# Self attention of a decoder layer: the softmax sums taken by ScalarE's accumulator from the first round's scores, in place of products with ones

## The chip, the cores and the metric

The kernel runs on 1 core of one Trainium2 chip. The metric is the device time of one execution in microseconds. Before the change the median of six executions is 4011.06 us (4002.22 to 4021.87). The profile and all times "in order of time" below come from one further execution, which took 4023.55 us with a span of 4021.6 us.

## The reference, cut to what matters

A decoder layer in float32: self attention, cross attention, a mixture of experts. Only self attention is touched. It is a differential attention over 32 sequences (b) of 128 tokens with 512 features, 16 heads of two halves ("sides") each, 16 features wide; a causal mask; for each side a softmax over the keys, and the second side's weights, times a scalar, are subtracted from the first's.

```python
q = (x @ Wq).reshape(b, t, 2 * H, HD).transpose(0, 2, 1, 3) * scaling
k = (x @ Wk).reshape(b, t, 2 * H, HD).transpose(0, 2, 1, 3)
v = (x @ Wv).reshape(b, t, H, 2 * HD).transpose(0, 2, 1, 3)
scores = jnp.einsum('bhqd,bhkd->bhqk', q, k)
aw = jax.nn.softmax((scores + causal).astype(jnp.float32), axis=-1)
aw = aw.reshape(b, H, 2, t, t)
aw = aw[:, :, 0] - lam * aw[:, :, 1]
attn = jnp.einsum('bhqk,bhkd->bhqd', aw, v)
attn = attn * jax.lax.rsqrt(jnp.mean(attn * attn, axis=-1, keepdims=True) + 1e-05)
```

## The kernel before, in words

`self_attention` handles one sequence b in two steps (cp = 0 and 1), eight heads a step, so there are 64 steps, and one step in two finishes a sequence. A step works on 4 head groups j (32 partitions each) times 2 chunks c times 2 sides: 16 score matrices of 128 queries by 128 keys. The scores are computed twice:

- First round, `maxima` (L231): eight products (L238) give scores with queries on partitions, in two PSUM buffers. VectorE (DVE in the profile) adds the causal mask and writes them to the SBUF tile `s` (L244), then takes the negated maximum of each row into `nm` (L251). `s` is read by nothing else.
- `turn_maxima` (L256): TensorE (PE) transposes `nm` (L262), and DVE puts the maxima into spare rows of the queries, `qm` (L264), so that the second round's products come out with the maximum already subtracted.
- Second round, `exponentials` (L270): 16 products (L279) give scores with keys on partitions; ScalarE (ACT) takes the exponential out of PSUM into `e`, two instructions (L286); GpSimd (POOL) zeroes what the mask excludes, two selects (L289).
- `weigh` (L294): eight products of `e` with the values (L303), and eight with `ones` (L309), which give the sum of the exponentials of each query. All land in one PSUM buffer `po`; DVE transposes it in blocks of 32 into `u` (L314).
- `divide` (L319): reciprocal of the sums (L323), the scalar for the second side (L324), and the product with the weighted values into `o` (L327).
- `finish` (L333), once a sequence: sum of the sides `at` on POOL (L338), squares `sq` on ACT (L342), their sums `ms` and a scaling on DVE (L344, L345), the power -0.5 `rr` on POOL (L347); `scale_out` gives `an` on DVE (L353), `turn_out` transposes it to `anT` (L361), `leave` multiplies by `wo` (L374) and adds the residual into `xres` (L378).

Beside these a step projects queries and keys of the next group of two sequences (`queries_and_keys`: products L207, evacuated by ACT to `kz` and `qT`, L213 and L218, and by POOL to `k1`, L214), projects values in every second step (`values`: L225, evacuated by ACT, L229), and normalizes and transposes inputs (`measure` with the moments of L56 to L66, `normalize` L74, `turn_in` L83 and L194).

The loop at the end of `self_attention` is a pipeline over steps n: step n does the maxima of step n, the exponentials of n - 1, weighing and dividing of n - 2, and so on up to `leave` of n - 5. The order on each engine is made from this program order by a scheduler that may move instructions; within an engine the instructions then run in that order, each waiting for semaphores of others. All PSUM results come from one pool of four buffers of two banks each, handed out in rotation, so a new product may have to wait for whoever empties the buffer used four requests earlier. In the last eight steps parts of cross attention are already mixed in.

Of the kernel before, what the change touches and what calls it, by code (L numbers as in the profile page):

```python
# [10 lines left out]
F32 = mybir.dt.float32  # L11
I32 = mybir.dt.int32
AF = mybir.ActivationFunctionType
# [5 lines left out]
P = 128  # L19
# [83 lines left out]
def self_attention(cm, x, x1_d, Wq, Wk, Wv, Wo, lq1, lk1, lq2, lk2, heads, heads_in, beside):  # L103
# [14 lines left out]
    nc, tc, bank = cm.nc, cm.tc, cm.banks  # L118
    B = x.shape[0]
    H, D, G = 16, 32, 2  # L120
    CP = 2
    ROW = (16, 0)
    with ExitStack() as ctx:
        wp = ctx.enter_context(tc.tile_pool(name="a_w", bufs=1))
        p1 = ctx.enter_context(tc.tile_pool(name="a_p1", bufs=1))
        p2 = ctx.enter_context(tc.tile_pool(name="a_p2", bufs=2))
# [44 lines left out]
        nc.scalar.activation(begun, cm.mhalf[:, 0:1], AF.Exp)  # L171

        hT, qT, kz, k1, vs = {}, {}, {}, {}, {}
        h, qm, expd, u, o, an = {}, {}, {}, {}, {}, {}

        def measure(b):
            if b < B:
# [42 lines left out]
        def values(g, i):  # L220
            if g * G >= B:
                return
            pv = bank()[:, 0, :]
            for ec in range(EC):
                nc.tensor.matmul(  # L225
                    pv, hT[g][:, ec, ts(i, P)], w["wv"][:, ec, :], start=ec == 0, stop=ec == EC - 1
                )
            vs[g, i] = p2.tile([P, E], F32, name="v", bufs=3)
            nc.scalar.copy(vs[g, i], pv)  # L229

        def maxima(b, cp):  # L231

            g, i = divmod(b, G)
            sc = [bank() for _ in range(2)]
            for c in range(CP):
                for j in range(4):
                    rows, oc = ts(j, 32), CP * cp + c
                    nc.tensor.matmul(  # L238
                        sc[j // 2][:, j % 2, ts(c, 2 * P)],
                        qT[g][rows, oc, i, :], kz[g, oc][rows, i], start=True, stop=True,  # L240
                    )
            s = p1.tile([P, 4, CP, 2, P], F32, name="s")
            for pair in range(2):
                nc.vector.tensor_tensor(  # L244
                    s[:, 2 * pair : 2 * pair + 2].rearrange("p j c s k -> p (j c s) k"),
                    sc[pair].rearrange("p j (x k) -> p (j x) k", k=P),
                    causal.unsqueeze(1).broadcast_to([P, 4 * CP, P]), ALU.add,
                )
            for side in range(2):
                at = nm[(CP * b + cp) % 2][:, side].rearrange("p (j r) -> p j r", r=32)  # L250
                nc.vector.tensor_reduce(  # L251
                    at[:, :, ROW[side] : ROW[side] + CP], s[:, :, :, side, :], AX.X, ALU.max,
                    negate=True,
                )

        def turn_maxima(b, cp):  # L256

            g, i = divmod(b, G)
            tr = bank()[:, 0, 0 : 2 * P].rearrange("p (s x) -> p s x", s=2)
            qm[b, cp] = p2.tile([P, 2, CP, P], F32, name="qm")  # L260
            for side in range(2):
                nc.tensor.transpose(tr[:, side], nm[(CP * b + cp) % 2][:, side], cm.ident)  # L262
            for side in range(2):
                nc.vector.scalar_tensor_tensor(  # L264
                    qm[b, cp][:, side], qT[g][:, CP * cp : CP * cp + CP, i, :],
                    others[:, side : side + 1],
                    tr[:, side].unsqueeze(1).broadcast_to([P, CP, P]), ALU.mult, ALU.add,
                )

        def exponentials(b, cp):  # L270

            g, i = divmod(b, G)
            sc = [bank() for _ in range(2)]
            q = qm.pop((b, cp))
            for c in range(CP):
                for side in range(2):
                    for j in range(4):
                        rows, oc = ts(j, 32), CP * cp + c
                        nc.tensor.matmul(  # L279
                            sc[j // 2][:, j % 2, ts(2 * c + side, P)],  # L280
                            k1[g, oc][rows, i, side, :], q[rows, side, c, :], start=True, stop=True,
                        )
            for pair in range(2):
                e = pe.tile([P, 2, CP, 2, P], F32, name="e")
                flat = e.rearrange("p j c s q -> p (j c s) q")
                nc.scalar.activation(  # L286
                    flat, sc[pair].rearrange("p j (x q) -> p (j x) q", q=P), AF.Exp
                )
                nc.gpsimd.affine_select(  # L289
                    out=flat, in_=flat, compare_op=ALU.is_ge, fill=0.0, base=0,  # L290
                    pattern=[[0, 4 * CP], [1, P]], channel_multiplier=-1,
                )
                expd[b, cp, pair] = e

        def weigh(b, cp):


            g, i = divmod(b, G)
            po = bank()
            es = [expd.pop((b, cp, pair)) for pair in range(2)]  # L300
            for c in range(CP):
                for j in range(4):
                    nc.tensor.matmul(  # L303
                        po[ts(j, 32), 0, ts(c, 2 * P)], vs[g, i][:, ts(4 * (CP * cp + c) + j, D)],
                        es[j // 2][:, j % 2, c], start=True, stop=True,
                    )
            for c in range(CP):
                for j in range(4):
                    nc.tensor.matmul(  # L309
                        po[ts(j, 32), 1, 0 : 2 * P], ones[:, c, :], es[j // 2][:, j % 2, c],  # L310
                        start=c == 0, stop=c == CP - 1,
                    )
            u[b, cp] = p1.tile([P, 6, 4, D], F32, name="u")
            nc.vector.transpose(  # L314
                u[b, cp].rearrange("p n k d -> p (n k d)"),
                po.rearrange("p two n -> p (two n)")[:, 0 : 6 * P],
            )

        def divide(b, cp):  # L319

            t = u.pop((b, cp))
            rs = p2.tile([P, CP, 2, 4], F32, name="rs")
            nc.vector.reciprocal(rs.rearrange("p c s k -> p s k c"), t[:, 4:6, :, 0:CP])  # L323
            nc.vector.tensor_scalar(rs[:, :, 1, :], rs[:, :, 1, :], nlam, None, ALU.mult)  # L324
            if cp == 0:
                o[b] = p1.tile([P, 2 * CP, 2, 4 * D], F32, name="o")
            nc.vector.tensor_tensor(  # L327
                o[b][:, CP * cp : CP * cp + CP].rearrange("p c s (k d) -> p (c s k) d", d=D),
                t[:, 0:4].rearrange("p n k d -> p (n k) d"),
                rs.rearrange("p c s k -> p (c s k)").unsqueeze(2).broadcast_to([P, 8 * CP, D]),  # L330
                ALU.mult,
            )
# [64 lines left out]
            )  # L397
        nc.vector.tensor_scalar(others, others, -1.0, 1.0, ALU.mult, ALU.add)


        ones = wp.tile([P, CP, D], F32, name="a_ones")
        nc.vector.memset(ones, 0.0)
        for c in range(CP):
            nc.vector.memset(ones[:, c, c : c + 1], 1.0)

        for b in range(G):
            measure(b)

# [9 lines left out]


        nm = [wp.tile([P, 2, P], F32, name=f"a_nm{i}") for i in range(2)]  # L420
        for t in nm:
            nc.gpsimd.memset(t, 0.0)

        for b in range(G):
# [26 lines left out]
        for n in range(len(steps) + 5):  # L451
            g, k = divmod(n, 2 * G)
            if n == len(steps) - 2 * G:
                early.close()
            at = {ago: steps[n - ago] for ago in range(6) if 0 <= n - ago < len(steps)}
            if 1 in at:
                turn_maxima(*at[1])
            if 0 in at:
                maxima(*at[0])
            queries_and_keys(g + 1, k)  # L460
            if 1 in at:
                exponentials(*at[1])
            if 2 in at:
                weigh(*at[2])
            if k % 2:
                values(g + 1, k // 2)
            elif 5 in at:
                leave(at[5][0])
            if 3 in at and at[3][1]:
                scale_out(at[3][0])  # L470
            if 2 in at:
                divide(*at[2])
                if at[2][1]:
                    finish(at[2][0])
            b = (g + 2) * G + k // 2
            if k % 2 == 0:
                measure(b)
                if 4 in at:
                    load_again(at[4][0])
            else:  # L480
                normalize(b)
                turn_in(b)
                load(b + G)
                if 4 in at:
                    turn_out(at[4][0])
            if n in beside:
                beside[n]()


class CrossAttention:  # L490
# [19 lines left out]
    ROW = (16, 0)  # L510
# [1158 lines left out]
```

## Time and profile before

| | us |
|---|---|
| median of six executions | 4011.06 |
| lowest and highest | 4002.22, 4021.87 |
| profiled execution | 4023.55 |
| its span | 4021.6 |
| self attention alone | about 0 to 770 of the span |
| self attention with cross attention mixed in | about 770 to 860 |
| granted TensorE clock, mean over the span | 0.991 |
| L309, products with ones, mean of one record | 0.379 (two records a product, four products side by side) |
| L286, exponential 128 x 1024 on ACT | 1.021 |
| L314, transpose 128 x 768 on DVE | 0.978 |

A line of a group in the profile names the source line, the engine, the operation, output and inputs, the shapes, the count, then busy time in us and the mean of one in ns, then the idle time of the engine before them and who ended it. In the view in order of time a line has start and length in us, the engine, the source line, the operation, the count of merged records and, in brackets, the idle time ahead and its releaser. A float32 product shows as two records, a transpose as one.

### The profile page before, as it was taken

How to read it: one execution, taken by the hardware profiler on the slowest of the kernel's cores; microseconds unless marked ns; L12 is line 12 of the kernel's file. 1: busy time of each engine (PE TensorE's matmuls, PEld its weight loads, DVE VectorE, ACT ScalarE, POOL GpSimd, SP SyncE). 2: the span in 40 equal slices, each digit the busy share in tenths (PEclk: the TensorE clock that was granted, in tenths of full speed). 3: DMA queues.
4: the chain of work that ended last, by engine and by line, in shares of the span. 5: the costliest groups of instructions: out<-in, count | busy, mean ns of one | idle time of the engine just before them, and what ended most of it. 6: DMA issues, size and time to landing. Idle time of an engine off the chain costs nothing. (4 is left out here: it accounts for less than half of the span.)

```text
span 4021.6 us, 58171 instructions
## 1 busy us (share of the span) xinstructions
PE 3869.6 (96%) x20020; PEld 2029.2 (50%) x20020; DVE 2201.1 (55%) x3525; ACT 1191.4 (30%) x1696; POOL 2255.8 (56%) x2420
## 2 busy tenths in 40 slices
PE   8999999989999999999999999999999999999999
PEld 5666666533333333334445555555555555555444
DVE  5777777778888888888323333333333333333111
ACT  3333333235665555555301111111111111111000
POOL 4444444453666666665326777777777777775000
PEclk9999999989999999999999999999999999999999
DMA  3110110121111111111145767676766676676210
GB/s 107 33 33 27 33 32 27 33 84 40 59 56 51 48 48 48 48 45 37 61 135 140 178 153 182 140 187 147 173 156 164 163 176 152 160 165 152 85 63 32
DMA packets 285980, 387.22 MB, mean 96 GB/s; under 512 B 147888, under 2 KB 179248, under 8 KB 285616
## 3 DMA queue, kind: packets, MB, share of 16 engines
q0 software_dynamic: 62912, 109.85, 15.3%
q1 hardware_dynamic: 81792, 190.98, 14.9%
q10 hardware_dynamic: 140976, 82.60, 7.4%
q8 instruction: 162, 2.65, 0.3%
q14 instruction: 138, 1.13, 0.1%
HBM read 617.52 MB, written 143.07 MB: 189 GB/s over the span
## 5 line engine op out<-in xcount | busy, mean ns | idle before, releaser
L1381 POOL DMA_INDIRECT e_xr<-h_d,e_run_of x832 | 849.5, 1021 | 288.7 <-issue 263.6
L1411 DVE TENSOR_TENSOR e_gu<-e_act,ps 128x352 f32<-128x352 f32 x208 | 108.4, 521 | 994.2 <-ACT e_act L1410 557.0
L653 DVE TENSOR_REDUCE nm<-ps 128x2 f32<-128x1024 f32 x512 | 610.9, 1220 | 61.5 <-PE ps L649 55.6
L1442 PE MATMUL ps<-wd,e_guT 128*128 128x512 f32 (+1 forms) x1248 | 577.0, 598 | 30.9 <-ACT e_y L1446 12.0
L676 ACT ACTIVATE xp<-ps 128x1024 f32<-128x1024 f32 x512 | 510.3, 1022 | 282.3 <-PE ps L649 213.7
L672 PE MATMUL ps<-xqn,xk 32*128 32x512 f32 x2048 | 537.9, 623 | 20.2 <-ACT xp L676 19.6
L1406 PE MATMUL ps<-wg,e_xT 128*128 128x352 f32 x1664 | 529.9, 461 | 15.0 <-DMA wg<-in_L_ffn_w_gate_dram 11.3
L649 PE MATMUL ps<-xk,xq 32*128 32x512 f32 x2048 | 537.1, 628 | 1.5 <-DVE xres L378 1.4
L1406 PE MATMUL ps<-wu,e_xT 128*128 128x352 f32 x1664 | 528.9, 461 | 7.0 <-DMA wu<-in_L_ffn_w_up_dram 5.8
L1406 PEld LDWEIGHTS ps<-wg,e_xT 128*128 128x128 f32 x1664 | 315.2, 190 | 253.9 <-issue 112.5
L1447 POOL DMA_INDIRECT sum_d<-e_y,e_into x208 | 338.1, 1625 | 178.3 <-ACT e_y L1446 96.3
L1406 PEld LDWEIGHTS ps<-wu,e_xT 128*128 128x128 f32 x1664 | 316.8, 191 | 186.5 <-DMA wu<-in_L_ffn_w_up_dram 9.1
L1442 PEld LDWEIGHTS ps<-wd,e_guT 128*128 128x128 f32 (+1 forms) x1248 | 236.3, 191 | 285.5 <-issue 225.9
L1410 ACT ACTIVATE e_act<-ps 128x352 f32<-128x352 f32 x208 | 96.3, 463 | 949.4 <-PE ps L1406 390.8
L672 PEld LDWEIGHTS ps<-xqn,xk 32*128 32x128 f32 x2048 | 165.2, 183 | 243.2 <-ACT xp L676 99.2
L1446 ACT ACTIVATE e_y<-ps,e_weight 128x512 f32<-128x512 f32 x208 | 142.9, 687 | 421.2 <-PE ps L1442 248.1
L1432 DVE STREAM_TRANSPOSE e_guT<-e_gr 96x384 f32<-96x384 f32 (+1 forms) x416 | 230.4, 554 | 61.5 <-DMA e_gr<-e_gu_d 49.6
L687 PE MATMUL ps<-xp,v 128*32 128x512 f32 x2048 | 246.0, 598 | 8.8 <-ACT xp L676 8.7
L987 POOL DMA_INDIRECT table_d<-entry,at x192 | 196.5, 1023 | 71.2 <-issue 50.8
L1393 DVE STREAM_TRANSPOSE e_xT<-e_xr 128x512 f32<-128x512 f32 x208 | 226.5, 1089 | 12.5 <-DMA e_xr<-h_d,e_run_of 8.6
L214 POOL TENSOR_SCALAR k<-kz,a_keep,a_extra 128x256 f32<-128x256 f32 x128 | 69.8, 554 | 265.3 <-ACT kz L213 265.3
L649 PEld LDWEIGHTS ps<-xk,xq 32*128 32x128 f32 x2048 | 161.2, 183 | 31.0 <-issue 9.7
(267 smaller groups left out, 4963.8 us busy)
## 6 DMA issues: line engine op xcount, KB each, us to landing
wg<-in_L_ffn_w_gate_dram SPq DMA_DIRECT2D x208, 704.0 KB
wu<-in_L_ffn_w_up_dram SPq DMA_DIRECT2D x208, 704.0 KB
wd<-in_L_ffn_w_down_dram SPq DMA_DIRECT2D x208, 576.0 KB
e_gu_d<-e_gu ACTq DMA_DIRECT2D x208, 192.0 KB
e_gr<-e_gu_d ACTq DMA_DIRECT2D x208, 192.0 KB
wd<-in_L_ffn_w_down_dram SPq DMA_DIRECT2D x208, 128.0 KB
e_xr<-h_d,e_run_of POOLq DMA_INDIRECT x832
xres<-in_x_dram SPq DMA_DIRECT2D x32, 256.0 KB
```

What stands on the lines that cost most here:

```text
L649: self.nc.tensor.matmul(sc[:, i, :], q[rows, ts(c, P)], k[rows, :], start=True, stop=True)
L653: self.nc.vector.tensor_reduce(at[:, self.ROW[side], 2 * pair : 2 * pair + 2], sc, AX.X, ALU.max, negate=True)
L672: self.nc.tensor.matmul(sc[:, i, :], k[rows, ts(c, P)], q[rows, :], start=True, stop=True)
L676: self.nc.scalar.activation(e, sc, AF.Exp)
L687: self.nc.tensor.matmul(po[b, side][ts(j, 32), :], self.v2[b % 2][:, c, 2 * j + side, :], es[j // 2][:, j % 2, :], start=c == 0, stop=c == ...
L987: self.nc.gpsimd.indirect_dma_start(out=self.table_ds[k % 2][:, :], out_offset=bass.IndirectOffsetOnAxis(ap=self.at[b][:, k : k + 1], axis=0),
L1381: self.cm.nc.gpsimd.indirect_dma_start(out=xr[:, t, :], out_offset=None, in_=self.h3_d.rearrange("t (q f) -> (t q) f", q=self.Q), in_offse ...
L1393: self.cm.nc.vector.transpose(xT.rearrange("p c (t i) -> p c t i", t=self.Q), self.xr.pop(i).rearrange("p t (j c) -> p c t j", c=EC),)
L1406: nc.tensor.matmul(pgu[:, half, 0:M], t[:, c, :], w[:, c, :], start=c == 0, stop=c == EC - 1)
L1432: self.cm.nc.vector.transpose(t[rows, 0:n, :].rearrange("p c (t i) -> p c t i", t=self.Q), g[rows, :, 0 : 32 * n].rearrange("p t (j c) -> ...
L1442: nc.tensor.matmul(py, t[:n, c, :], self.wd[s][:n, c, :], start=c == 0, stop=c == len(M_CHUNKS) - 1)
L1447: nc.gpsimd.indirect_dma_start(out=self.sum_d[:, :], out_offset=bass.IndirectOffsetOnAxis(ap=self.into[:, i : i + 1], axis=0), in_=y[:, :] ...
```

## The change

The exponentials of the first round's scores are now taken too, from `s` in place, by ScalarE: 16 activations of 128 x 128 a step, one for each score matrix, with the negated maximum as bias (one value a partition) and the engine's accumulator giving the row's sum into a column of a new tile `sm` (two of them, used in turn). `weigh` transposes `sm` into the free bank of `po` with one TensorE transpose; the eight products with `ones` and the tile `ones` go. The DVE transpose into `u` is 640 columns wide in place of 768. `s` moves to a pool with two buffers. In program order the sums of chunk 0 come behind `turn_maxima`, those of chunk 1 behind `exponentials`, both for step n - 1.

```diff
-            s = p1.tile([P, 4, CP, 2, P], F32, name="s")
+            s = sc_of[b, cp] = p2.tile([P, 4, CP, 2, P], F32, name="s")
...
+        def sums(b, cp, c):
+            n = (CP * b + cp) % 2
+            s = sc_of[b, cp]
+            for j in range(4):
+                for side in range(2):
+                    at = 32 * j + ROW[side] + c
+                    to = 32 * j + 2 * c + side
+                    nc.scalar.activation(
+                        s[:, j, c, side, :], s[:, j, c, side, :], AF.Exp,
+                        bias=nm[n][:, side, at : at + 1], accum_out=sm[n][:, to : to + 1],
+                    )
+            if c == CP - 1:
+                del sc_of[b, cp]
...
-            for c in range(CP):
-                for j in range(4):
-                    nc.tensor.matmul(
-                        po[ts(j, 32), 1, 0 : 2 * P], ones[:, c, :], es[j // 2][:, j % 2, c],
-                        start=c == 0, stop=c == CP - 1,
-                    )
-            u[b, cp] = p1.tile([P, 6, 4, D], F32, name="u")
+            nc.tensor.transpose(po[:, 1, 0:P], sm[(CP * b + cp) % 2], cm.ident)
+            u[b, cp] = p1.tile([P, 5, 4, D], F32, name="u")
             nc.vector.transpose(
                 u[b, cp].rearrange("p n k d -> p (n k d)"),
-                po.rearrange("p two n -> p (two n)")[:, 0 : 6 * P],
+                po.rearrange("p two n -> p (two n)")[:, 0 : 5 * P],
             )
...
-            nc.vector.reciprocal(rs.rearrange("p c s k -> p s k c"), t[:, 4:6, :, 0:CP])
+            nc.vector.reciprocal(rs.rearrange("p c s k -> p k (c s)"), t[:, 4, :, 0 : 2 * CP])
...
+        sm = [wp.tile([P, P], F32, name=f"a_sm{i}") for i in range(2)]
+        for t in nm + sm:
             nc.gpsimd.memset(t, 0.0)
...
             if 1 in at:
                 turn_maxima(*at[1])
+                sums(*at[1], 0)
             if 0 in at:
                 maxima(*at[0])
             queries_and_keys(g + 1, k)
             if 1 in at:
                 exponentials(*at[1])
+                sums(*at[1], 1)
```

More of the change, by code (lines that the diff above doesn't have):

```diff
@@ L173, in self_attention @@
         hT, qT, kz, k1, vs = {}, {}, {}, {}, {}
-        h, qm, expd, u, o, an = {}, {}, {}, {}, {}, {}
+        h, sc_of, qm, expd, u, o, an = {}, {}, {}, {}, {}, {}, {}
         def measure(b):
@@ L398, in self_attention @@
         nc.vector.tensor_scalar(others, others, -1.0, 1.0, ALU.mult, ALU.add)
[L401 to L404, printed above, removed]
         for b in range(G):
@@ L420, in self_attention @@
         nm = [wp.tile([P, 2, P], F32, name=f"a_nm{i}") for i in range(2)]
-        for t in nm:
+        sm = [wp.tile([P, P], F32, name=f"a_sm{i}") for i in range(2)]
+        for t in nm + sm:
             nc.gpsimd.memset(t, 0.0)
```

## Prediction

> **What bounds the kernel now.** I read the page first (shares of busy time), then the table by stage, then the instructions in order of time over two steps of self attention, then the groups of ScalarE by form. The page says that TensorE is nearly always busy:
>
> ```profile
> PE 3869.6 (96%) x20020; PEld 2029.2 (50%) x20020; DVE 2201.1 (55%) x3525; ACT 1191.4 (30%) x1696; POOL 2255.8 (56%) x2420
> ```
>
> The table by stage (busy us and, in brackets, instructions of PE, PEld, DVE, ACT, POOL; then clock, DMA share, GB/s), cut to the steady part of self attention:
>
> ```profile
> 100.00:750.00 650.00, 635.51 (x5516) 406.31 (x5514) 501.54 (x711) 213.52 (x357) 288.42 (x299) 0.99 0.10 30
> ```
>
> PE 98%, ACT 33%. From this alone the change pays: it takes work from PE and gives it to an idle engine. The instructions in order of time say otherwise. The work repeats every two steps: L361's anT starts at 402.64 and again at 427.99, so a pair takes 25.35 us. From one pair (start, us, engine, line, operation, count):
>
> ```profile
> 408.74 0.98 DVE L314 STREAM_TRANSPOSE u<-ps 128x768 f32<-128x768 f32 x1 [0.78 <-PE ps L309]
> 409.76 0.26 DVE L323 RECIPROCAL rs<-u 128x16 f32<-128x16 f32 x1
> 410.05 0.23 DVE L324 TENSOR_SCALAR rs<-rs,nlam 128x8 f32<-128x8 f32 x1
> 410.32 0.69 DVE L327 TENSOR_TENSOR o<-u,rs 128x512 f32<-128x512 f32 x1
> 413.06 0.69 DVE L344 TENSOR_REDUCE ms<-sq 128x16 f32<-128x512 f32 x1 [2.04 <-ACT sq L342]
> ```
> ```profile
> 406.85 1.94 ACT L286 ACTIVATE e<-ps 128x1024 f32<-128x1024 f32 x2
> 407.63 1.05 PE L309 MATMUL ps<-e,a_ones 128*32 128x256 f32 x16
> 407.94 2.13 POOL L289 TENSOR_SCALAR_AFFINE_SELECT e<-e 128x1024 f32<-128x1024 f32 x2 [0.53 <-ACT e L286]
> 411.10 1.27 POOL L338 TENSOR_TENSOR at<-o 128x512 f32<-128x512 f32 x1 [1.02 <-DVE o L327]
> 412.39 0.63 ACT L342 ACTIVATE sq<-at 128x512 f32<-128x512 f32 x1 [3.61 <-POOL at L338]
> 414.03 2.92 POOL L347 TENSOR_TENSOR rr<-ms,mhalf 128x16 f32<-128x16 f32 x1 [1.67 <-DVE ms L345]
> 416.99 0.69 DVE L353 SCALAR_TENSOR_TENSOR an<-at,rr 128x512 f32<-128x512 f32 x1 [2.26 <-POOL rr L347]
> 418.26 1.76 PE L279 MATMUL ps<-qm,k 32*128 32x128 f32 x32
> 424.00 2.14 POOL L289 TENSOR_SCALAR_AFFINE_SELECT e<-e 128x1024 f32<-128x1024 f32 x2
> 424.28 0.84 DVE L324 TENSOR_SCALAR rs<-rs,nlam 128x8 f32<-128x8 f32 x1
> 425.16 1.53 DVE L327 TENSOR_TENSOR o<-u,rs 128x512 f32<-128x512 f32 x1
> 427.34 1.99 PE L207 MATMUL ps<-hT,wk 128*128 128x256 f32 x8 [0.39 <-DVE xres L378]
> ```
>
> PE's busy time holds waits. L279 takes 1.76 us in this step and 1.17 us at 405.64 in the step before, the same 32 records; L238 takes 1.79 at 412.89 and 1.15 at 400.45; and at 427.34 PE waits 0.39 for xres. That is 1.6 us of slack in each pair. What sets the pair is a ring: PE's exponential scores (405.64) → e on ACT (ends 408.8) → the select on POOL (407.94 to 410.07) → rs, o on DVE (410.05 to 411.01) → at on POOL (to 412.37) → sq on ACT → ms on DVE → rr on POOL (to 416.95) → an on DVE (416.99), behind which DVE is busy without a break to xres, which frees the bank for L207 at 427.34 → 3.65 us of projections → the next exponential scores (430.99 = 405.64 + 25.35).
>
> **The products with ones.** L309 starts at 407.63 and the next product at 408.61: 0.98 us of PE a step, two a pair. In their place is one transpose; the two of L262 stand 0.31 us apart from their successor (400.14 to 400.45), so 0.16 us, up to 0.3 with its entry: PE saves about 0.7 us a step. The ring does not go through L309 but beside it. With it gone u can start at 407.96 (end of DVE's reductions) and not 408.74, and takes 640 columns for 768 (0.98 × 5/6 = 0.82, by width). But rs would come at 409.05, inside the select. What happens then is in the other step: rs at 424.28, 0.28 us into a select, takes 0.84 us and not 0.23, and ends with the first select; o takes 1.53 and not 0.69, and ends 0.55 us after the second. So rs and o end at about 410.1 and 410.8, and 0.15 to 0.2 us of the 0.98 is kept. In the other step the select starts at 424.00, after ve on DVE, and holds rs whether u is 0.16 us shorter or not: nothing.
>
> The Trainium skill (SBUF — State Buffer, "Who interferes with whom") says of this that the pair of ports shared by VectorE and GpSimd is an exclusive lock, for two SBUF inputs or a two-port mode, and that the first to issue blocks the other. The rows above agree for rs and o. By its sentence that the order of issue decides, an earlier rs could also take the lock first, and the sum would then gain up to 0.8 us a pair; the sum here goes by the rows.
>
> **DVE's order.** As the changed kernel is built, DVE runs ms, one qm, then ms2 (L345) and the other qm; before it ran ms, ms2, qm, qm. The last steps of before have that order once: L344 at 793.25, L345 at 794.24, 0.99 us apart, against 413.06 to 413.78, 0.72. rr waits for ms2: +0.27 us a pair in the ring. bn_stats moves behind the reductions of its step; its aggregate then follows it at once: 0 to +0.15, I take +0.1. The second buffer for s takes a wait away that nobody shows; the wait of L244 for ScalarE is for sums of two steps ago, ended some 5 us or more ahead.
>
> **The 16 new activations a step.** Their own row is missing; alone, without accumulator, the nearest rows give it. ScalarE's groups by form:
>
> ```profile
> L213 ACT ACTIVATE kz<-ps,a_keep 128x256 f32<-128x256 f32 x128 | 53.6, 470 | 395.2 <-PE ps L207 395.1
> L218 ACT ACTIVATE qT<-ps 128x256 f32<-128x256 f32 x64 | 24.5, 383 | 0.0
> L342 ACT ACTIVATE sq<-at 128x512 f32<-128x512 f32 x32 | 20.2, 630 | 113.5 <-POOL at L338 113.5
> L905 ACT ACTIVATE score<-score 128x32 f32<-128x32 f32 x32 | 7.4, 230 | 39.9 <-DVE score L904 39.9
> L440 ACT ACTIVATE lam_exps<-lam_dots 128x2 f32<-128x2 f32 x1 | 0.2, 212 | 0.0
> ```
>
> sq less score: 400 ns for 480 columns, 0.833 a column; 128 columns from SBUF: 310. An operand per partition (kz less qT): +87, so 0.40 us. Neighbours overlap by 0.10 (two e take 1.94, one 1.021), so one every 0.30 us if the accumulator costs nothing: the low end. Should the sum need a second instruction to fetch it, the nearest row is ScalarE's shortest (212 ns). It cannot begin before its activation has ended, so it loses the overlap there, and I let the next activation overlap with it: 0.40 + 0.21 - 0.10 = 0.51. With no overlap at all: 0.61, the high end. I take 0.51, the case of the nearest row; no row shows an accumulator. The Trainium skill (VectorE: DVE Perf Modes, "Two Vector instructions with no wait between them") says of VectorE that an output of the accumulator is a second instruction; it says nothing of ScalarE, and no row shows it.
>
> ScalarE has 8.4 us a pair now (kz, kz, qT 1.10 and e, e 1.94 in each step; sq, v, hT, h 2.30): with 32 sums it is 18.0, 24.7 or 27.9 us, by 0.30, 0.51, 0.61, in 25.35. It runs in order, and as built a step with sq has seven sums between e and sq and nine between hT and h; the other step has sixteen between e and kz. Behind seven sums wait sq, v and hT, and on sq the ring. Free at 408.8 + 7 × 0.51 = 412.4; sq is due at 412.39 - 0.2: late by 0.2. The nine end at 414.2 + 4.6 = 418.8, h at 419.5, kz (due 418.4) late by 1.1: e then ends at 422.5 for 421.83, which POOL takes at 424.00 anyway, after ve. The sixteen end at 430.7, kz due 431.1. So at 0.51 ScalarE just keeps up.
>
> **Sum for a pair:** -0.2 (o) + 0.27 (ms2) + 0.1 (ve) + 0.2 (sq) = about +0.4 us. The steady part has (765 - 90) / 25.35 = 27 pairs: +11 us. The last steps (765 to 860) are bound by DVE and POOL waits; as built, sums stand ahead of e there (nine: 793.7 + 4.6 = 798.3 for 795.95) and of h, which now waits behind rot; 1.8 to 1.9 us products with ones at the low clock go. I take +5, between -3 and +10. All: +16 on the profiled execution (4023.55, span 4021.6), which is 12.5 above the median 4011.06 of six; on the median 4027.
>
> **Rivals.** A difference within 0.3% (12 us) cannot be told from none here.
> 1. ScalarE becomes the bound: above 0.55 us a sum, 8.4 + 32 × 0.55 = 26.0. At 0.61 the pair is 27.9 plus about 0.1: +2.6 × 27 = +70, tail +8: 4089. For: 0.61 is in the bounds, and the order has no slack. Against: neighbours overlap in every row. 0.28.
> 2. The other side, faster: PE's time counts after all. If rs and o take their turn ahead of the select, the ring shortens with PE; then 2 × 0.75 × 27 = 41 us go: 3970. For: 98% busy. Against: the waits inside L279, L238, L207 and rs's 0.84. It decides where rs starts before 409.0. 0.12.
> 3. The sums are cheap (0.30 to 0.42) and hidden, sq is not late: +0.17 × 27 + 3 = +8: 4019, no difference to be told. 0.18.
> Forecast: 0.42, itself 4013 to 4045, two thirds of it above 4023. Slower 0.28 + 0.28 = 0.56; same 0.14 + 0.18 = 0.32; faster 0.12. That the sums go to another engine or the products stay is ruled out by the instructions as built. The range 3998 to 4085 leaves out most of rival 2 and the top of rival 1.
>
> **What would show it.** Right: pairs of about 25.8 us, PE's L207 waiting about 1 us or more for xres where it waited 0.39, rs held by the select in both steps, sq starting right behind the seventh sum, ACT 90% busy or more. Wrong: pairs of 24 us with rs free of the select (rival 2); kz and e starting right behind sums, POOL and PE waiting for e, pairs over 26.5 us (rival 1); sq waiting for POOL as now (rival 3). A sum slower than 0.61 us would break the upper end.

## The result, and the profile after

The changed kernel takes 4019.87 us (median of 35 runs, 4002.70 to 4031.98) where the kernel before, measured beside it, takes 4009.01 us (72 runs, 3994.11 to 4021.87). The ratio is 1.0024, with a 95% interval of 1.0017 to 1.0031: slower by 0.24%, less than the 0.3% that the prediction called the edge of what can be told, but with an interval that lies above one. The profiled execution of the changed kernel took 4010.80 us (span 4008.8); that of before took 4023.55. So the two traces stand the other way round from the medians, and only stretches of them are compared here, not their ends.

The page of the changed kernel (busy time, share of the span and instructions of each engine), and from the table by stage the same stretch as before (busy us and instructions of PE, PEld, DVE, ACT, POOL; clock, DMA share, GB/s):

```profile
PE 3817.3 (95%) x19060; PEld 1998.1 (50%) x19060; DVE 2216.4 (55%) x3522; ACT 1587.7 (40%) x3744; POOL 2261.4 (56%) x2422
```
```profile
100.00:750.00 650.00, 590.41 (x4721) 375.75 (x4717) 512.69 (x707) 525.40 (x1970) 287.83 (x299) 1.00 0.10 30
```

PE works 45 us less in this stretch (635.51 before) and ScalarE 312 us more (213.52), and the pair is longer all the same: L372's anT starts at 409.70 and again at 435.42, 25.72 us, where it was 25.35. The groups of ScalarE by form (busy us, mean ns of one, idle time in front) show what a sum is:

```profile
L265 ACT ACTIVATE s<-s,a_nm 128x128 f32<-128x128 f32 x1024 | 396.0, 392 | 14.1 <-DVE a_nm L251 12.4 <-PE ps L323 1.7
L265 ACT ACTIVATION_READ_ACCUMULATOR s<-s,a_nm 128x1 f32 x1024 | 195.9, 191 | 0.0
```

Two instructions, and the second overlaps both its own activation and the next one. In order of time, one sum and the start of the next (0.38 us later; 13 in a row from 404.19 to 409.20 come 0.386 apart):

```profile
416.50 0.39 ACT L265 ACTIVATE s<-s,a_nm 128x128 f32<-128x128 f32 x1
416.79 0.20 ACT L265 ACTIVATION_READ_ACCUMULATOR s<-s,a_nm 128x1 f32 x1
416.88 0.39 ACT L265 ACTIVATE s<-s,a_nm 128x128 f32<-128x128 f32 x1
```

One pair of the changed kernel in that order, without the sums (start, us, engine, line, operation, count, wait):

```profile
409.05 1.99 PE L207 MATMUL ps<-hT,wk 128*128 128x256 f32 x8 [1.46 <-DVE xres L389]
...
412.70 1.17 PE L295 MATMUL ps<-qm,k 32*128 32x128 f32 x32
...
415.00 2.14 POOL L305 TENSOR_SCALAR_AFFINE_SELECT e<-e 128x1024 f32<-128x1024 f32 x2 [0.52 <-ACT e L302]
415.17 0.85 DVE L325 STREAM_TRANSPOSE u<-ps 128x640 f32<-128x640 f32 x1
...
416.35 0.82 DVE L335 TENSOR_SCALAR rs<-rs,nlam 128x8 f32<-128x8 f32 x1
...
417.20 0.69 DVE L338 TENSOR_TENSOR o<-u,rs 128x512 f32<-128x512 f32 x1
...
419.28 0.63 ACT L353 ACTIVATE sq<-at 128x512 f32<-128x512 f32 x1 [0.75 <-POOL at L349]
...
419.94 0.69 DVE L355 TENSOR_REDUCE ms<-sq 128x16 f32<-128x512 f32 x1 [2.05 <-ACT sq L353]
...
420.55 0.47 DVE L280 SCALAR_TENSOR_TENSOR qm<-qT,a_others,ps 128x256 f32<-128x256 f32 x1
...
420.93 0.17 DVE L356 TENSOR_SCALAR ms<-ms 128x16 f32<-128x16 f32 x1
...
424.14 0.69 DVE L364 SCALAR_TENSOR_TENSOR an<-at,rr 128x512 f32<-128x512 f32 x1 [2.65 <-POOL rr L358]
424.75 2.35 DVE L244 TENSOR_TENSOR s<-ps,causal 128x1024 f32<-128x1024 f32 x2
...
427.13 2.35 DVE L251 TENSOR_REDUCE a_nm<-s 128x8 f32<-128x1024 f32 x2
...
429.39 0.68 DVE L56 BATCH_NORM_STATS2 a_ln_stats<-xin 128x6 f32<-128x512 f32 x1
430.11 0.18 DVE L58 BATCH_NORM_AGGREGATE a_ln_mv<-a_ln_stats 128x2 f32<-128x6 f32 x1
...
431.43 2.14 POOL L305 TENSOR_SCALAR_AFFINE_SELECT e<-e 128x1024 f32<-128x1024 f32 x2
```

The step that has sq, ms and rr is called the odd step here, and the one behind it the other step. Measured from the exponential scores of the odd step (405.64 before, 412.70 after), each member of the ring stands so, in us:

| member of the ring | before | after | difference |
|---|---|---|---|
| o starts | 4.68 | 4.50 | -0.18 |
| sq starts | 6.75 | 6.58 | -0.17 |
| ms (second instruction) | 8.14 | 8.23 | +0.09 |
| an | 11.35 | 11.44 | +0.09 |
| select of the next step | 18.36 | 18.73 | +0.37 |
| pair | 25.35 | 25.72 | +0.37 |

Three terms make the difference, -0.18 at o, +0.27 at the second ms, +0.28 at the select, and PE's wait for xres at L207 grew from 0.39 to 1.46 us: the work that PE lost became waiting (PE shows no work in 59.6 of the 650 us, where it was 14.5).

### The profile page after: what moved, and what is told of

Read it like the earlier page. It is cut to its first block, busy times and chain, and to the rows that moved or that the text cites. A ratio compares the mean times of both kernels' runs of the same rounds, so it can differ in the third digit from the quotient of the medians.

```text
span 4008.8 us, 58380 instructions
## 1 busy us (share of the span) xinstructions
PE 3817.3 (95%) x19060; PEld 1998.1 (50%) x19060; DVE 2216.4 (55%) x3522; ACT 1587.7 (40%) x3744; POOL 2261.4 (56%) x2422
## 5 line engine op out<-in xcount | busy, mean ns | idle before, releaser
L1390 POOL DMA_INDIRECT e_xr<-h_d,e_run_of x832 | 852.0, 1024 | 283.1 <-issue 266.7
L1415 PE MATMUL ps<-wg,e_xT 128*128 128x352 f32 x1664 | 530.7, 461 | 14.7 <-DMA wg<-in_L_ffn_w_gate_dram 12.4
L265 ACT ACTIVATE s<-s,a_nm 128x128 f32<-128x128 f32 x1024 | 396.0, 392 | 14.1 <-DVE a_nm L251 12.4
```

Of the source, the lines that this page charges most:

```text
L265: nc.scalar.activation(s[:, j, c, side, :], s[:, j, c, side, :], AF.Exp, bias=nm[n][:, side, at : at + 1], accum_out=sm[n][:, to : to + 1],)
L1390: self.cm.nc.gpsimd.indirect_dma_start(out=xr[:, t, :], out_offset=None, in_=self.h3_d.rearrange("t (q f) -> (t q) f", q=self.Q), in_offse ...
L1415: nc.tensor.matmul(pgu[:, half, 0:M], t[:, c, :], w[:, c, :], start=c == 0, stop=c == EC - 1)
```

## The experiments

Theory: the ring sets the pair, PE does not, and the two places in DVE's order are what the change costs. Rivals: ScalarE's load; PE's saving counts, or the products that remain would. The kernels ran in four sets, each with runs of the kernel before on the same chip (medians 3966.18 of 23, 3966.73 of 9, 3956.01 of 23, 3967.91 of 11); times are compared within a set. "xp" is the start of cross attention's first exponentials in the trace, a mark for the end of self attention.

| run | set | median us | ratio to before (95%) | pair us | xp us |
|---|---|---|---|---|---|
| ms2_first | 1 | 3974.37 | 1.0020 (1.0010 to 1.0030) | 25.44 | 876.9 |
| ones_kept | 1 | 3980.97 | 1.0039 (1.0025 to 1.0053) | 25.72 | 887.7 |
| no_sums | 1 | 3966.47 | 0.9998 (0.9987 to 1.0008) | 25.17 | 865.8 |
| no_accum | 1 | 4087.41 | 1.0305 (1.0289 to 1.0320) | 28.6 to 29.4 | |
| an_late_before | 2 | 3924.29 | 0.9899 (0.9884 to 0.9914) | 24.17 | 838.2 |
| an_late_after | 2 | 3928.51 | 0.9902 (0.9888 to 0.9917) | 23.8 to 24.2 | 832.1 |
| sums_24 | 2 | 4026.56 | 1.0155 (1.0137 to 1.0172) | 26.4 to 27.3 | |
| xin_3 | 3 | 3897.94 | 0.9845 (0.9829 to 0.9862) | 23.19 | 813.1 |
| after_again | 3 | 3968.50 | 1.0031 (1.0021 to 1.0042) | 25.70 | 879.0 |
| before_again | 3 | one run, 3960.54 | | 25.35 | 875.2 |
| before_s2 | 3 | 3957.78 | 1.0001 (0.9990 to 1.0012) | 25.35 | 874.9 |
| xin_3_before | 4 | 3935.26 | 0.9900 (0.9881 to 0.9919) | 24.17 | 836.6 |

### ms2_first: the second ms ahead of qm

```diff
+        done = [None]
...
             for side in range(2):
-                nc.vector.scalar_tensor_tensor(
-                    qm[b, cp][:, side], qT[g][:, CP * cp : CP * cp + CP, i, :],
...
+                with tc.issue_after(done[0].ins) if done[0] else nullcontext():
+                    nc.vector.scalar_tensor_tensor(
+                        qm[b, cp][:, side], qT[g][:, CP * cp : CP * cp + CP, i, :],
...
-            nc.vector.tensor_scalar(ms, ms, 1.0 / D, EPS, ALU.mult, ALU.add)
+            done[0] = nc.vector.tensor_scalar(ms, ms, 1.0 / D, EPS, ALU.mult, ALU.add)
```

> The changed kernel with one edit of order: both qm of a step are queued behind ms2 (L345 of before) on VectorE, as they were before the change. Theory (ring through the select, at, sq, ms, ms2, rr, an; the order of VectorE is what the change paid for): ms to ms2 0.72 us instead of 0.99, the pair of steps 25.71 - 0.27 = 25.44 us, about 7 us off the changed kernel, a ratio to before of about 1.000 to 1.001. Rival (ScalarE's load of sums is what costs): the pair stays at 25.7, ratio 1.0024.

Its trace in order of time:

```profile
417.65 0.69 DVE L358 TENSOR_REDUCE ms<-sq 128x16 f32<-128x512 f32 x1 [2.05 <-ACT sq L356]
418.37 0.17 DVE L359 TENSOR_SCALAR ms<-ms 128x16 f32<-128x16 f32 x1
418.45 0.86 DVE L283 SCALAR_TENSOR_TENSOR qm<-qT,a_others,ps 128x256 f32<-128x256 f32 x2
```

0.72 us from ms to ms again, where the changed kernel has 0.99, and the pair is 25.44, shorter by 0.28. One qm in front of one small instruction costs its 0.27 us in full at the end of the pair. The median did not follow (1.0020, expected 1.000 to 1.001); with after_again it is told how little the traces say about that.

### ones_kept: the sums and the products with ones

```diff
+            for c in range(CP):
+                for j in range(4):
+                    nc.tensor.matmul(
+                        po[ts(j, 32), 1, 2 * P : 4 * P], ones[:, c, :], es[j // 2][:, j % 2, c],
+                        start=c == 0, stop=c == CP - 1,
+                    )
             nc.tensor.transpose(po[:, 1, 0:P], sm[(CP * b + cp) % 2], cm.ident)
...
```

> The changed kernel that also keeps the eight products with ones a step, into columns that nobody reads. The scheduler puts ms2 ahead of qm here, as before, and bn_stats behind the reductions, as after the change. Theory: the products lie beside the ring, so the pair is 25.35 + 0.27 (bn_stats) + 0.0 (select and u as balanced as before) = 25.6 us, no slower than the changed kernel, ratio 1.002. Rival (TensorE's time counts): 2 x 0.75 us more than the changed kernel, pair 27.2, ratio about 1.012.

The pair is 25.72 us, to the hundredth the changed kernel's, but this is two terms that cancel. PE does more work (624.6 us busy in 100 to 750, for 590.4), and u does wait for it:

```profile
416.13 0.85 DVE L331 STREAM_TRANSPOSE u<-ps 128x640 f32<-128x640 f32 x1 [1.01 <-PE ps L329]
...
417.58 0.69 DVE L344 TENSOR_TENSOR o<-u,rs 128x512 f32<-128x512 f32 x1
```

Measured from the exponential scores (412.80 here), o starts at 4.78, where the changed kernel has 4.50: +0.28. Against that the second ms stands directly behind the first here, as the expectation says: -0.27. The fair comparison is ms2_first, which has the same order on DVE and lacks the products: 25.72 against 25.44. So in the steady pairs the products cost 0.28 us, all of it at o, and not the 1.5 us of the rival; the expected 25.6 took o as it stood before the change (4.68), but the transpose of the sums now stands behind the products. Ratio 1.0039: the late pairs, where PE counts for more (below), pay too.

### no_sums: the gain without the price

```diff
             if 1 in at:
                 turn_maxima(*at[1])
-                sums(*at[1], 0)
...
                 exponentials(*at[1])
-                sums(*at[1], 1)
...
+        for t in sm:
+            nc.gpsimd.memset(t, 1.0)
```

> The changed kernel without the 16 activations a step: the sums are left out, a constant tile is transposed in their place. So TensorE loses its products and ScalarE gains nothing. VectorE's order is that of before in both places. Theory: only o comes 0.18 us earlier, pair 25.35 - 0.18 = 25.17 us, ratio about 0.999. Rival (TensorE's time counts): 2 x 0.7 us a pair go, pair 23.9, ratio 0.990.

The pair is 25.17: the change without its activations is worth 0.18 us a pair, the term of o, although the products' 2 us a pair are gone from PE. Here DVE's order is that of the kernel before in both places (ms, ms, qm, qm; bn_stats between the masking adds and the reductions): the sums reach DVE through the planned order alone. The rival of 23.9 us (PE's saving counts in full) fell.

### no_accum: the sums without the accumulator

```diff
-                        bias=nm[n][:, side, at : at + 1], accum_out=sm[n][:, to : to + 1],
+                        bias=nm[n][:, side, at : at + 1],
...
+        for t in sm:
+            nc.gpsimd.memset(t, 1.0)
```

> The changed kernel with the 16 activations but without their accumulator output: the sums are left out, a constant tile is transposed. VectorE's order is that of before in both places. Theory: each activation takes 0.30 us (0.386 with the accumulator), ScalarE is busy about 18 of 25 us, and since ScalarE is not late anywhere the pair is as without any sums, 25.17 us, ratio about 0.999. Rival (ScalarE's load costs): the pair lies between 25.3 and 25.7, ratio 1.000 to 1.002.

This missed: less work on ScalarE made the pair 28.6 to 29.4 us, and the kernel 3% slower than before. The group of its activations, and two lines in order of time:

```profile
L265 ACT ACTIVATE s<-s,a_nm 128x128 f32<-128x128 f32 x1024 | 319.9, 399 | 325.4 <-DVE a_nm L251 325.4
```
```profile
416.55 0.40 ACT L265 ACTIVATE s<-s,a_nm 128x128 f32<-128x128 f32 x1 [7.06 <-DVE a_nm L251]
416.86 0.82 ACT L213 ACTIVATE kz<-ps,a_keep 128x256 f32<-128x256 f32 x2
```

A single sum of the next step now stands in front of kz (in the other step three, which wait 3.29 us at 398.79). It waits 7.06 us for DVE's maxima, and kz, qT and e wait behind it; over the kernel such waits come to 325 us. Why the planned order puts a sum there was not tried. This is the mechanism of the prediction's first rival (kz and e behind sums), reached by the order and not by the load. So the run says nothing of what the accumulator costs in the ring; that two neighbouring activations without it come 0.29 us apart (seven take 2.15 us at 400.66 of this trace) is what it shows of the price, for 0.386 with it.

### sums_24: half as many sums again

```diff
-                    nc.scalar.activation(
-                        s[:, j, c, side, :], s[:, j, c, side, :], AF.Exp,
-                        bias=nm[n][:, side, at : at + 1], accum_out=sm[n][:, to : to + 1],
-                    )
+                    for out in ([again[:, side, :]] if j % 2 else []) + [s[:, j, c, side, :]]:
+                        nc.scalar.activation(
+                            out, s[:, j, c, side, :], AF.Exp,
+                            bias=nm[n][:, side, at : at + 1], accum_out=sm[n][:, to : to + 1],
+                        )
...
+        again = wp.tile([P, 2, P], F32, name="a_again")
```

> The changed kernel with 24 activations a step in place of 16: half of them are taken twice, once into a tile that nobody reads. Theory (0.386 us a sum, ScalarE in order): 8.4 + 48 x 0.386 = 26.9 us a pair, more than the ring's 25.7, so ScalarE becomes the bound: pair 27 us, 8 us x 0.386 x ... in all 27 pairs x 1.3 = 35 us over the changed kernel, ratio to before 1.011. Rival (ScalarE was the bound already at 16): 16 x 0.386 = 6.2 us a pair more, pair 31.9, ratio 1.04.

With 48 sums a pair the pair is 26.4 to 27.3 us, 26.9 in the mean: 8.4 + 48 × 0.386 = 26.9, and ScalarE is busy 391.31 of the 400 us from 200 to 600. There ScalarE is the bound, as rival 1 has it, and at 32 sums (8.4 + 12.4 = 20.8 of 25.72 us) it is not. The ratio, 1.0155 (1.0137 to 1.0172), is above the 1.011 that was expected; its mean clock was 0.988 for 0.994 of before.

### an_late_before and an_late_after: the ring cut

In both kernels an is put behind the second reduction on DVE, so that DVE no longer stands still for rr (2.26 us a pair before, 2.65 after). The same edit in each:

```diff
-                nc.vector.tensor_reduce(
+                cm.reduced = nc.vector.tensor_reduce(
...
-            nc.vector.scalar_tensor_tensor(
-                an[b], at, 1.0 - LAMBDA_INIT, rr.unsqueeze(2).broadcast_to([P, H, D]),
-                ALU.mult, ALU.mult,
-            )
+            with tc.issue_after(cm.reduced.ins):
+                nc.vector.scalar_tensor_tensor(
+                    an[b], at, 1.0 - LAMBDA_INIT, rr.unsqueeze(2).broadcast_to([P, H, D]),
+                    ALU.mult, ALU.mult,
+                )
```

> The kernel before with one edit of order: an (L353) is queued behind the reductions of its step on VectorE, instead of ahead of the additions of the mask, which stood behind it waiting for rr on GpSimd. No work is changed. Theory: the ring loses the wait for rr (2.3 us); TensorE, 23.5 us of work a pair plus its entry into the ring, becomes the bound: pair 24.0 to 24.3, about 30 us off, ratio 0.992. Rival (TensorE bound all along, 98 percent busy): nothing, ratio 1.000.

> The changed kernel with the same edit of order. Theory: the ring no longer hides what TensorE saves, so now the missing products count: TensorE has 22.1 us a pair, pair 23.2 to 23.5, 60 us off the changed kernel, ratio to before 0.986, and about 0.9 us a pair below the kernel before with the same edit, where the change alone lost 0.36. Rival (sums on ScalarE bind once the ring is shorter: 20.7 us of work in order): pair above 24, no better than the kernel before with the edit.

The kernel before drops to a pair of 24.17 us and 0.9899 of its time (0.992 was expected) by a change of order alone. This shows the ring: not one instruction went, and PE, busy 390.15 of 400 us before, does the same work in 1.18 us less a pair. The changed kernel did not come down to 23.2 to 23.5 as expected, but to 23.8 to 24.2, about 0.2 us below an_late_before, and its median shows no gain over it (0.9902 and 0.9899). Its trace:

```profile
400.92 0.81 ACT L74 ACTIVATE h<-xin,a_ln_down,a_ln_rstd 128x512 f32<-128x512 f32 x1
...
404.42 0.69 DVE L56 BATCH_NORM_STATS2 a_ln_stats<-xin 128x6 f32<-128x512 f32 x1 [0.80 <-DMA xin<-in_x_dram]
...
405.37 0.15 DVE L60 TENSOR_SCALAR a_ln_ve<-a_ln_mv 128x1 f32<-128x1 f32 x1
...
405.60 0.55 POOL L62 TENSOR_TENSOR a_ln_rstd<-a_ln_ve,mhalf 128x1 f32<-128x1 f32 x1 [1.55 <-DVE a_ln_ve L60]
...
406.46 2.14 POOL L305 TENSOR_SCALAR_AFFINE_SELECT e<-e 128x1024 f32<-128x1024 f32 x2
```

As the waits have it: h stands behind nine sums on ScalarE; it frees the buffer for the next block, whose load comes late; bn_stats waits 0.80 us for it; ve follows, POOL's rstd waits for ve, and the select stands behind rstd and holds rs and o in its turn.

### xin_3 and xin_3_before: a third buffer for xin

Each is the kernel above with one more edit:

```diff
-            xin[b] = pj2.tile([P, E], F32, name="xin")
+            xin[b] = pj2.tile([P, E], F32, name="xin", bufs=3)
```

> The kernel of an_late_after with a third buffer for xin (the loads of self attention start a block earlier; nothing else of the order in the loop is moved). Theory: what lengthened an_late_after's pair to about 23.95 us is DVE's bn_stats waiting 0.80 us for xin, whose load was late since h, which frees the buffer, stood behind nine sums on ACT. Then the wait at bn_stats goes, the select moves ahead by about 0.7 us, and the pair is 23.2 to 23.5 us; self attention ends some 27 x 0.6 = 16 us earlier (first xp at 812 to 820 us where it was 832), ratio to before 0.985 to 0.987. Rival: the sums hold the pair by ACT's order itself (v and sq behind them), the load was only the last of several waits: pair 23.8 to 24.0, ratio 0.990 as an_late_after.

> The kernel before with the same two edits as xin_3 (an behind the second reduction, a third buffer for xin), so that the products with ones stand against the sums with the ring out of the way. Theory: with the ring shorter PE is the bound, which in an_late_before was busy 399.1 of 400 us at a pair of 24.17 us; a third buffer cannot help it, so pair 24.1 to 24.2, first xp about 838, ratio 0.988 to 0.991, and what xin_3 has over it (23.19 against 24.17, 0.98 us a pair) is the products' own. Rival: the third buffer is what made xin_3 short, whatever the sums are made of: pair 23.2 to 23.5, ratio 0.984 to 0.986.

Pair 23.19 us and ratio 0.9845 (0.9829 to 0.9862) for the changed kernel: the fastest of the study. But the reason given with it was half wrong. bn_stats still waits for the load (16.4 us in 200 to 600, for 12.2 in an_late_after). What went is the next link: bn_stats runs a block further ahead, POOL's rstd is no longer queued behind the ve of the same step and stands well ahead of the select, so a late load holds nobody. The kernel before gains nothing from the third buffer (24.17, as in an_late_before). The table by stage of the two, xin_3_before first, xin_3 second:

```profile
200.00:600.00 400.00, 399.33 (x3571) 253.65 (x3570) 311.73 (x472) 137.10 (x229) 191.99 (x199) 1.00 0.11 34
```
```profile
200.00:600.00 400.00, 389.56 (x3202) 249.54 (x3204) 328.61 (x488) 354.91 (x1343) 204.92 (x206) 1.00 0.11 35
```

With the products PE is busy 399.33 of 400 us and is the bound. Its busy time still holds a wait (L238 takes 1.79 us once a pair, and 1.15 in the other step), so the share alone does not prove it; what does is that the pair falls by 0.98 us when the products go and by nothing with the buffer alone. Without them it is not full even at a pair 0.98 us shorter; what is left of its idle time is 9.8 us of waiting for v behind sq. So the change is worth 0.98 us a pair once the ring is out of PE's way, and self attention ends 23.5 us sooner (xp 813.1 for 836.6). The two were timed in different sets, on different chips, each against before: 0.9845 and 0.9900.

### after_again, before_again and before_s2: both kernels on one chip, and the place of the buffers

The first two have no edit. before_s2 is the kernel before with the second buffer of s; its instructions stand in the same order:

```diff
-            s = p1.tile([P, 4, CP, 2, P], F32, name="s")
+            s = p2.tile([P, 4, CP, 2, P], F32, name="s")
```

> The changed kernel as it is, on the chip of the other experiments. Theory that the pair is the whole change: pair 25.72 us, first xp some 4 to 8 us later than before's, ratio as measured first, 1.0024 (1.0017 to 1.0031). Rival: the changed kernels lose 6 to 13 us more somewhere behind self attention on this chip, as the difference of median and first xp of the other runs suggests: ratio 1.004 to 1.005.

> The kernel before once more, for its trace on this chip: pair 25.35 us, first xp at about 879 us, granted clock 0.994 to 0.995 over the span.

> The kernel before with the masked scores s in two buffers, as the changed kernel has them; every engine's order is the kernel before's, and no sum moves. Theory that the place of the buffers alone costs what the changed kernels lose behind self attention: pair 25.35 us and first xp as before, but ratio 1.002 to 1.003. Otherwise: pair 25.35, ratio 1.000 (0.999 to 1.001), or below if the second buffer lets the masking adds start earlier, which the chain of waits of before does not show.

The pairs are 25.70 and 25.35 again, and the ratio of after_again, 1.0031 (1.0021 to 1.0042), settles neither for the theory (up to 1.0031) nor for the rival (1.004 to 1.005). From the two traces of this chip the change adds up like this (starts of anT, after less before): +4.85 us up to the first, +0.67 in the first pair, +7.34 in the next 21, then -7.18 in the last nine: 5.7 at the last anT. xp stands 3.8 us later. What happens in the last pairs is seen at xres, in order of time, in before_again and then in after_again:

```profile
725.90 0.69 DVE L378 TENSOR_TENSOR xres<-xres,ps 128x512 f32<-128x512 f32 x1 [1.20 <-PE ps L374]
```
```profile
736.73 0.69 DVE L389 TENSOR_TENSOR xres<-xres,ps 128x512 f32<-128x512 f32 x1 [0.53 <-PE ps L385]
```

The input is used up, so bn_stats and ve are gone, the select is early, and DVE waits for PE: now the ring does go through PE, and without the products it is shorter by 0.65 us a pair (24.95 to 24.30). ones_kept has 25.12 in these pairs and ms2_first 24.03, so there the products are worth 1.09. This is four of the nine pairs (-2.7 in all); another -2.55 falls in one single pair with cross attention mixed in, and was not followed further. The first 4.85 us come from the activations: the first anT of no_sums stands at 84.73 and that of ones_kept at 88.75, for 84.62 and 89.47 here.

The medians of this chip differ by 12.5 us. The two traced executions differ by 3.7 (3964.26 and 3960.54), and that is what they differ by at xp already: behind xp they take the same time. So the other 8.7 us of the medians are in no trace, and where they lie is not shown. The stretch behind xp varies by itself: 3074.7 us in before_s2 and 3085.4 in before_again (time less xp), with the same instructions. before_s2 (1.0001) rules out the place of the buffers.

The granted clock over the whole run is lower in the changed kernel, 0.9925 in the mean of its 12 runs for 0.9945 in the 23 of before; among those 23 runs a thousandth of clock goes with 3.3 us, so that 0.0020 would be 6.5 us, an estimate that may hold part of the 3.8. In the traces the lower clock stands in good part ahead of xp: 0.91 and 0.87 in 780 to 820 and 820 to 860 before, 0.89 and 0.80 after (each is the mean of its stretch). There PE has stood still for longer than in the steady pairs, and the products behind take nearly twice their 1.07 us: 1.94 behind a wait of 4.19 us (before_again, L303 at 795.42), 1.93 behind one of 3.31 (after_again, L319 at 803.68). Every kernel of the table without the products has a lower mean clock than the kernel before beside it (by 0.0007 in xin_3 to 0.0166 in no_accum), and none with them by more than 0.0004. Whether this is the cause was not tried and stays open.

## Why the prediction was right, and where it was not

**The bound: right.** That PE at 98% does not set the pair, and that the ring through POOL, ScalarE and DVE does, is shown three ways: no_sums takes the products' 2 us a pair from PE and gains 0.18; ones_kept gives them back and loses 0.28 against ms2_first; an_late_before removes no instruction and gains 1.18. "The ring does not go through L309 but beside it" is right for the size and not quite for the path: u waits for L309 in the odd step (0.78 us before), and what the products are worth in the steady pairs comes through that wait, at o.

**o, -0.2: right,** -0.18. u starts 0.63 us earlier in the odd step (0.78 forecast) and rs lands inside the select as the other step had shown (0.82 us, for 0.84 there). The Trainium skill (SBUF — State Buffer, "Who interferes with whom") says that the first to issue blocks the other. In the steady pairs the select is the first in both steps, so the 0.8 us a pair that the sentence would have allowed did not come; no run here shows rs taking the lock. The other order may be seen once in the last steps of before: an, two inputs from SBUF, starts 0.07 us behind a select (797.43), takes 1.57 us for 0.69, and the two selects take 2.59 us for 2.14, as if the second had waited for an.

**The second ms, +0.27: right,** +0.27, and ms2_first takes it away alone (25.72 to 25.44).

**ve, +0.1 (0 to +0.15): too small,** +0.28 (ve is L60, for which POOL's rstd and behind it the select wait). The step that failed is the count of what bn_stats (L56) leaves behind when it moves: "its aggregate then follows it at once". The same stretch before the change:

```profile
417.60 2.35 DVE L244 TENSOR_TENSOR s<-ps,causal 128x1024 f32<-128x1024 f32 x2
419.86 0.68 DVE L56 BATCH_NORM_STATS2 a_ln_stats<-xin 128x6 f32<-128x512 f32 x1
420.46 2.33 DVE L251 TENSOR_REDUCE a_nm<-s 128x8 f32<-128x1024 f32 x2
422.71 0.17 DVE L58 BATCH_NORM_AGGREGATE a_ln_mv<-a_ln_stats 128x2 f32<-128x6 f32 x1
```

Here bn_stats stood between the adds (L244) and the reductions (L251), which read what the adds write, and the reductions between bn_stats and its aggregate (L58). DVE started each neighbour that did not depend on the last about 0.1 us before that one's end: adds to bn_stats 2.26, bn_stats to reductions 0.60. Now the reductions follow the adds at 2.38 and the aggregate follows bn_stats at 0.72: twice 0.12, where the prediction had at most one such gap; the rest of the 0.28 is a few hundredths behind the aggregate. No run moves bn_stats alone; the size is read from these rows, and it fits the 0.27 us between no_sums (25.17) and ms2_first (25.44), which differ in this order and in the sums.

**A sum, 0.51 us (0.30 to 0.61): too dear,** 0.386. The second instruction was guessed right (0.191, for 0.21 from a row of 212 ns; the shortest of before, L171, has 203), but the step "cannot begin before its activation has ended" failed: it starts 0.29 us into an activation of 0.39 and so overlaps with its own activation too, so it costs about 0.09 over the 0.29 without it. The Trainium skill (VectorE: DVE Perf Modes, "Two Vector instructions with no wait between them") says of VectorE that an output of the accumulator is a second instruction; this trace shows the same on ScalarE, 1024 times.

**sq late by 0.2: wrong,** none. sq waits 0.75 us for POOL, as the third rival has it, since seven sums take 2.7 us and not 3.6. ScalarE is 81% busy (525.40 of 650), not 90%. So rival 3 was right about the sums and the forecast about the rest: -0.18 + 0.27 + 0.28 = +0.37 a pair where the forecast had +0.4. Two sizes missed in opposite ways (ve by +0.18, sq by -0.2), so that the pair came out by luck as much as by the working.

**The sum, +16: near, and partly by luck.** Forecast: 27 pairs × 0.4 = +11, last steps +5. In the traces of one chip: first steps +4.85 and +0.67, which the sum did not have; 21 pairs, +7.34; last nine -7.18, where +5 was put (bounds -3 to +10). There "bound by DVE and POOL waits" was the step that failed: in the pairs that were followed DVE waits for PE's L374. The medians of that chip have 8.7 us more, which the sum did not have either and no trace shows. At the first measurement this came to 4019.87 - 4009.01 = +10.9: within the range, nearer to the 4019 of rival 3 than to the forecast's 4027, and on the side of no difference that the text could tell rather than of the slower that it held likelier.

**The rivals.** Rival 1 (ScalarE the bound) does not hold at 32 sums but does at 48 (sums_24), and by its order in no_accum. Rival 2 (PE's time counts) does not hold in the steady pairs, where 0.18 us came of it; by other routes than the one it names, PE counts in the late pairs and in xin_3. Which engine binds is a matter of little more than a microsecond: the ring stands at 25.35 us and PE, with the products, at 24.17.

## What to carry to other kernels

Before taking work from the busiest engine, find in the order of time who waits for it: here 98% busy held waits, and taking the products out of it bought 0.18 us a pair (no_sums) and, with the sums in their place, nothing, while an order in which one instruction no longer waits for POOL bought 1%. Do that first, with the third buffer for xin, and the same change is worth 0.98 us a pair. New instructions on an idle engine cost most, here, through the in-order queues: look at what they now stand in front of (h, kz) and at what the planner moved on other engines because of them (ms, bn_stats). When a control has the expected time, see that no two terms cancel in it, as in ones_kept. And count stages apart: the start, the steady pairs and the last ones had +5.5, +7.3 and -7.2 us.

## What the runs showed of the hardware

- ScalarE's accumulator: ACTIVATE 0.392 and ACTIVATION_READ_ACCUMULATOR 0.191 us, one sum every 0.386 us; without accumulator one every 0.29.
- DVE started an independent neighbour about 0.1 us before the last one's end; a dependent one came 0.12 us later (2.38 for 2.26, 0.72 for 0.60). Moving bn_stats cost this gap twice.
- A 128x8 tensor_scalar took 0.23 us beside no select and 0.82 to 0.98 under one; the 128x512 product of two SBUF operands 0.69 and 1.53.
- Products of 1.07 us took 1.94 and 1.93 behind waits of TensorE of 4.19 and 3.31 us (before_again, after_again).
- The mean granted clock differed between kernels whose instructions differ in one stage only: in the third set 0.9945 before and 0.9925 after, in the first 0.9944 before and 0.9778 in no_accum (means over the runs).
